# Layer 2's edge products as two float32r parts, its leaky relu as a linear sum plus one relu, and TensorE's order written out

## The chip, the cores and the metric

The kernel runs on one core of a Trainium2 chip. Its engines work side by side, each through its own queue of instructions in order: TensorE (PE, with its weight loads shown apart as PEld) writes matmul results to PSUM banks; VectorE (DVE) and ScalarE (ACT) read PSUM and SBUF; GpSimd (POOL) works on SBUF and starts some transfers; SyncE (SP) starts the others. The metric is the device time of one execution in microseconds, lower is better. Before the change it is 2248.09 us, the median of three runs (2247.92 to 2248.36).

## The reference, cut to what matters

Four graph layers run one after the other over x of 128 x 64 x 256, each followed by a residual and a layer norm. The change lies in layer 2, an attention over the 512 edges (src, dst) of a graph of 64 nodes, with 4 heads of 64 columns:

```python
Xq = (H @ W_lin.T).reshape(bt, n, h, dh)
Xv = (H @ W_val.T).reshape(bt, n, h, dh)
Qs = Xq[:, src]
Kt = Xq[:, dst]
e = jnp.einsum('behd,hd->beh', jax.nn.leaky_relu(Qs + Kt, 0.2), a)
e = e + jnp.log(A0[src, dst] + EPS)[None, :, None]
...
attn = ex / denom[src]
...
return Y @ W_out.T
```

So for every graph, edge and head a score is needed: the sum over 64 columns of a times leaky_relu(Xq[src] + Xq[dst]). The softmax over the edges of a source node and the weighted sum of Xv follow. All of it is float32.

## The kernel before, in words

The rows of x (two graphs of 64 nodes fill the 128 partitions) are held in SBUF as a tile X of NT = 64 slices. Layer 2 goes over them in K = 32 steps k of two slices i = 0, 1. The generator `scores` runs one step each time it is called on; its parts are these.

- `transposed(k)` transposes the two slices on TensorE (L2134, four 128x128 transposes into one PSUM bank of the tag "m") and DVE copies them to xT (L2136).
- `maps(k, xT)` multiplies xT by W_lin and W_val side by side (L2146, four matmuls of 128x512 into two banks "m"). ACT copies the first half of a bank to xq (L2150) and the second to xv (L2160), and SP stores xv in DRAM (L2161) for the second part of the layer.
- `edges(c)` for one half c of the 256 columns: for each slice i and each graph b of a slice, a matmul of the 64 rows of xq with the table GG (L2183), whose 512 columns hold a one at an edge's source node and a one at its target. The result is Xq[src] + Xq[dst], 128 columns on the partitions by 512 edges, in PSUM (tag "l", two tiles of two banks). ACT copies each to xs in SBUF (L2188), and DVE makes max(0.2 x, x) of it there (L2189), the leaky relu.
- `products` multiplies xs with az (L2122), the vector a spread so that each matmul adds its scores to the right rows of a bank "sc". After 16 steps a bank holds the scores of half the graphs.

The banks are shared out by pools: two for "m", four for "l", two for "sc". A bank is given to the next user in turn, who waits until the last one has been read.

The order of a step is that of the loop in `scores`. In the first steps (`apart` before, `early` after; the generator it shares the time with ends after step 14) `run(*beside)` puts pieces of layer 1's last normalization, `last_pass`, in between: ACT scales y (L2038), TensorE transposes it (L2047, into banks "m"), DVE adds it to X (L1349), takes the statistics (L1352, L1353) and, for four slices at a time, works out scale and shift (L1271 on DVE, a square root L1273 on ACT, L1274 to L1277 and L1364 on DVE), and ACT applies them (L1368, four rows). From step 15 on other work is called beside the steps: `softmax` of the first half (L2225 to L2269, which ends in scatters that POOL starts), `fetch` (L2279, M2 read back from DRAM by SP and POOL), and from step 25 on `values` (L2286 to L2329). Then layer 3 follows.

In what order an engine's instructions finally stand is decided by a scheduler, which keeps to data dependences and to the dependences added by hand: `after` makes the first product of a group wait for all of its operands, so that a wait is not met in the middle of a group, and `last` ties a group of score products behind the last edge product.

Of the kernel before, what the change touches and what calls it, by code (L numbers as in the profile page):

```python
# [7 lines left out]

F32 = mybir.dt.float32
I32 = mybir.dt.int32  # L10
# [1364 lines left out]
def tile_adj_resnorm(ctx: ExitStack, tc: tile.TileContext, I: dict, out: bass.AP, layers: int = 4):  # L1375
    nc = tc.nc
    v, s, te = nc.vector, nc.scalar, nc.tensor
# [10 lines left out]
    for b in range(2):  # L1388
        r, o = slice(b * N, (b + 1) * N), slice((1 - b) * N, (2 - b) * N)
# [9 lines left out]
    X = const.tile([P, NT, D], F32, tag="X", name="X")  # L1399
# [6 lines left out]
    ident = load("ident", [P, P], I["ident"], s)  # L1406
# [487 lines left out]
    NQ = NT // 4  # L1894
# [136 lines left out]
    def last_pass():  # L2031

        ln = Norm(nc, sy, X, 8, act=True)

        def normed(h):
            y = sy.tile([P, 2, 2 * P], F32, tag="y", name="y")
            for c in range(2):
                s.activation(y[:, c, :], Y[h // 2][:, c, h % 2 * 2 * P : (h % 2 + 1) * 2 * P], AF.Identity,  # L2038
                             bias=sh2[:, c : c + 1], scale=sc2[:, c : c + 1])
            return y  # L2040

        y = normed(0)
        for h in range(2 * NQ):
            ps = pp.tile([P, 512], F32, tag="m", name="m")
            for i in range(2):
                for c in range(2):
                    te.transpose(ps[:, i * D + c * P : i * D + (c + 1) * P], y[:, c, i * P : (i + 1) * P], ident)  # L2047
            with in_order(v, h < 3):
                ln.add(2 * h, ps, 2)
            if h == 1:  # L2050
                keep_awake(pg.tile([P, 2, 512], F32, tag="l", name="l")[:, 0, :], 2)
# [18 lines left out]
    with ExitStack() as l2:  # L2070
# [7 lines left out]
        edge_s = lt.tile([P, WE], F32, tag="edge_s", name="edge_s")  # L2078
        nc.sync.dma_start(edge_s, edge_d)
        GG, OS, lg, br, OE, ix = edge_tables(edge_s)  # L2080
        heads = lt.tile([P, 2], F32, tag="heads", name="heads")
        s.dma_start(heads, I["heads"].rearrange("p (h n) -> p h n", n=N)[:, :, 0])
        acol = lt.tile([P, 2], F32, tag="acol", name="acol")
# [9 lines left out]
        for c in range(2):  # L2093
            for h in range(2):
                o = (h + 1) * HU - 1
                v.tensor_tensor(az[:, c, o : o + 1], heads[:, h : h + 1], acol[:, c : c + 1], ALU.mult)
        bf, bb = br[:, :E], br[:, 1:]
        sc, M2 = [[None, None], [None, None]], [None, None]

        xvd = [dl.tile([P, 2, D], F32, tag=f"xv{k}", name=f"xv{k}") for k in range(NT // 2)]  # L2100

        taken, drawn, last = {}, {}, []
        beside = [iter(())]
        soft = []

        def after(ins, those, how=mybir.DependencyClass.Sync):
            for i in those:
                tc.add_manual_dep(ins.ins, i.ins.name, mybir.DependencyInfo(how, mybir.DependencyReason.DATA),
                                  reason="together")

        def products(todo, held):

            xss = [held.pop(x) for x in todo]
            mms = []
            for (k, c), (xs, _) in zip(todo, xss):
                half, u_ = divmod(k, HU)
                if u_ == 0:
                    sc[half][c] = pc.tile([P, 512], F32, tag="sc", name="sc")
                for b in range(2):
                    for i in range(2):  # L2120
                        q = 32 * (2 * b + i)
                        mms.append(te.matmul(sc[half][c][q : q + 32, :], az[:, c, HU - 1 - u_ : 3 * HU - 1 - u_],  # L2122
                                             xs[b, i], start=(u_ == 0), stop=(u_ == HU - 1)))
# [3 lines left out]
            after(mms[0], last[-1:], mybir.DependencyClass.NoSync)  # L2127

        def transposed(k):

            ps = pp.tile([P, 512], F32, tag="m", name="m")
            for i in range(2):
                for c in range(2):
                    te.transpose(ps[:, i * D + c * P : i * D + (c + 1) * P], X[:, 2 * k + i, c * P : (c + 1) * P], ident)  # L2134
            xT = sx.tile([P, 2, 2, P], F32, tag="xT", name="xT", bufs=1)
            v.tensor_copy(xT.rearrange("p i c n -> p (i c n)"), ps)  # L2136
            return xT

        def maps(k, xT, apart=False):

            xq, xv = [], sx.tile([P, 2, D], F32, tag="xv", name="xv")
            pss = [pp.tile([P, 512], F32, tag="m", name="m") for _ in range(2)]

            def product(i, cols):
                for c in range(2):
                    te.matmul(pss[i][:, cols], xT[:, i, c, :], wqv[:, c, cols], start=(c == 0), stop=(c == 1))  # L2146

            def first(i):
                xq.append(sx.tile([P, D], F32, tag="xq", name="xq", bufs=4))
                drawn[i] = s.copy(xq[i], pss[i][:, :D])  # L2150

            if apart:
                for i in range(2):
                    product(i, slice(0, D))
                    first(i)
            for i in range(2):
                product(i, slice(D, 2 * D) if apart else slice(0, 2 * D))
                if not apart:
                    first(i)
                s.copy(xv[:, i, :], pss[i][:, D:])  # L2160
            nc.sync.dma_start(xvd[k], xv)  # L2161
            return xq

        def scores():


            K = NT // 2
            xT = transposed(0)
            xq = maps(0, xT, True)
            next(beside[0])  # L2170
            next(beside[0])
            xT = transposed(1)


            held = {}

            def edges(c):
                xs, ready = {}, []
                for i in range(2):
                    pl = pg.tile([P, 2, 512], F32, tag="l", name="l")  # L2180
                    for b in range(2):
                        r = slice(b * N, (b + 1) * N)
                        mm = te.matmul(pl[:, b, :], xq[i][r, c * P : (c + 1) * P], GG[r, :], start=True, stop=True)  # L2183
                        if not b:
                            after(mm, taken.pop(i, []) + ([drawn[i]] if c == 0 else []))
                    for b in range(2):
                        x = xs[b, i] = sx.tile([P, E], F32, tag="xs", name="xs", bufs=10)
                        taken.setdefault(i, []).append(s.copy(x, pl[:, b, :]))  # L2188
                        ready.append(v.scalar_tensor_tensor(x, x, 0.2, x, ALU.mult, ALU.max))  # L2189
                held[k, c] = xs, ready  # L2190
                last.append(mm)

            for k in range(K):
                apart, xn = k < NQ, None
                edges(0)
                if apart:
                    run(*beside)
                    if k:
                        products([(k - 1, 1)], held)
                if k < K - 1:  # L2200
                    xn = maps(k + 1, xT)
                if apart:
                    run(*beside)
                elif k < K - 2:
                    xT = transposed(k + 2)
                edges(1)
# [126 lines left out]
        def run(*steps):  # L2333
            for x in steps:
                next(x, None)
# [172 lines left out]
```

## Time and profile before

| what | before |
|---|---|
| median of three runs | 2248.09 us |
| the profiled execution | 2244.9 us |
| its span, first to last instruction | 2243.1 us |
| mean granted TensorE clock | 0.995 |
| scoring of layer 2, first maps to last score products | about 1682 to 2049 us |

The profile is one execution. Its page gives busy time by engine (1), the span in 40 slices (2), the DMA queues (3), the chain of waits that ended last (4), and the costliest groups of instructions by line (5); other views cut out a stretch of time, or list instructions in order. A row "L2183 PE MATMUL l<-edge_s,xq ... x512 | 128.7, 616 | 0.4" says: line 2183, on TensorE, writing tile l from tiles edge_s and xq, 512 records, 128.7 us in which at least one of them ran, 616 ns for one, and 0.4 us of idle time of the engine in front of them. Records that overlap count once in the busy time. GG is a part of the tile edge_s and appears under that name.

### The profile page before, as it was taken

How to read it: one execution, taken by the hardware profiler on the slowest of the kernel's cores; microseconds unless marked ns; L12 is line 12 of the kernel's file. 1: busy time of each engine (PE TensorE's matmuls, PEld its weight loads, DVE VectorE, ACT ScalarE, POOL GpSimd, SP SyncE). 2: the span in 40 equal slices, each digit the busy share in tenths (PEclk: the TensorE clock that was granted, in tenths of full speed). 3: DMA queues.
4: the chain of work that ended last, by engine and by line, in shares of the span. 5: the costliest groups of instructions: out<-in, count | busy, mean ns of one | idle time of the engine just before them, and what ended most of it. 6: DMA issues, size and time to landing. Idle time of an engine off the chain costs nothing. (4 is left out here: it accounts for less than half of the span.)

```text
span 2243.1 us, 29992 instructions
## 1 busy us (share of the span) xinstructions
PE 2197.8 (98%) x8816; PEld 1211.7 (54%) x8816; DVE 1811.0 (81%) x9283; ACT 935.8 (42%) x1727; POOL 162.4 (7%) x196
## 2 busy tenths in 40 slices
PE   8999999999999999999999999999999999999997
PEld 6445665445665445665445654554434333446887
DVE  5788887888898899888899998877957777656688
ACT  1432322433322333332333322434427876567675
POOL 0111111111000000000000000000000000100631
PEclk9999999999999999999999999999999999999999
DMA  7001010111010111010111000012210100321522
GB/s 234 22 19 38 1 39 1 38 47 48 1 38 1 38 38 57 1 38 1 38 38 57 1 20 19 20 54 105 83 39 24 38 32 24 92 60 44 158 86 78
DMA packets 44667, 101.55 MB, mean 45 GB/s; under 512 B 5296, under 2 KB 23856, under 8 KB 43216
## 3 DMA queue, kind: packets, MB, share of 16 engines
q1 hardware_dynamic: 38384, 84.64, 11.0%
q0 software_dynamic: 3984, 14.40, 2.3%
q8 instruction: 70, 1.15, 0.2%
q10 hardware_dynamic: 2128, 0.54, 0.1%
q14 instruction: 101, 0.83, 0.1%
HBM read 67.97 MB, written 31.59 MB: 44 GB/s over the span
## 5 line engine op out<-in xcount | busy, mean ns | idle before, releaser
L1739 PE MATMUL pq<-H,wi 128*128 128x512 f32 (+1 forms) x1952 | 780.8, 540 | 1.5 <-ACT gate L1779 1.3
L1779 ACT ACTIVATE gate<-pq,bl 128x512 f32<-128x512 f32 (+1 forms) x504 | 315.8, 632 | 616.1 <-PE pq L1755 502.4
L1739 PEld LDWEIGHTS pq<-H,wi 128*128 128x128 f32 x1952 | 365.8, 190 | 337.5 <-issue 270.4
L1755 PE MATMUL pq<-lh,wh 128*128 128x512 f32 (+1 forms) x1152 | 462.8, 529 | 0.9 <-DVE lh L1797 0.8
L1755 PEld LDWEIGHTS pq<-lh,wh 128*128 128x128 f32 x1152 | 218.7, 190 | 203.0 <-issue 144.0
L2189 DVE SCALAR_TENSOR_TENSOR xs<-xs 128x512 f32<-128x512 f32 x256 | 165.2, 686 | 70.2 <-ACT xs L2188 69.2
L1782 ACT ACTIVATE gate<-lc 128x512 f32<-128x512 f32 (+1 forms) x144 | 83.6, 580 | 278.6 <-DVE lc L1794 103.2
L2188 ACT COPY xs<-l 128x512 f32<-128x512 f32 x256 | 134.1, 596 | 53.8 <-PE l L2183 43.8
L2183 PE MATMUL l<-edge_s,xq 64*128 64x512 f32 x512 | 128.7, 616 | 0.4 <-ACT xs L2188 0.3
L2146 PE MATMUL m<-wqv,xT 128*128 128x512 f32 (+1 forms) x264 | 121.8, 597 | 2.8 <-DVE X L1349 1.9
L2011 PE MATMUL ps<-h,w 128*128 128x512 f32 x256 | 115.9, 610 | 4.9 <-ACT h L2005 2.7
L1368 ACT ACTIVATE X<-X,ln_sh,ln_rs 128x256 f32<-128x256 f32 x187 | 97.5, 593 | 40.0 <-DVE ln_sh L1364 30.4
L1957 PE MATMUL ps<-at,w 128*128 128x512 f32 x256 | 113.2, 593 | 0.0
L802 POOL PARTITION_ALL_REDUCE qQ<-qSG x62 | 74.0, 1193 | 508.1 <-DVE pc L134 274.8
L2146 PEld LDWEIGHTS m<-wqv,xT 128*128 128x128 f32 x264 | 46.4, 189 | 76.6 <-issue 36.0
L2011 PEld LDWEIGHTS ps<-h,w 128*128 128x128 f32 x256 | 49.0, 195 | 65.7 <-issue 55.9
L1957 PEld LDWEIGHTS ps<-at,w 128*128 128x128 f32 x256 | 47.2, 190 | 52.8 <-issue 51.4
L2183 PEld LDWEIGHTS l<-edge_s,xq 64*128 64x128 f32 x512 | 44.5, 186 | 56.9 <-issue 41.7
L1352 DVE BATCH_NORM_STATS2 ln_st<-X 128x6 f32<-128x256 f32 x192 | 73.1, 416 | 1.2
L1797 DVE TENSOR_TENSOR lh<-gate 128x512 f32<-128x512 f32 (+1 forms) x72 | 43.0, 602 | 33.1 <-ACT gate L1779 33.1
L130 DVE SCALAR_TENSOR_TENSOR CS<-GA,qE 64x1 f32<-64x1 f32 x294 | 61.7, 210 | 9.5
L130 DVE SCALAR_TENSOR_TENSOR GA<-qtg,CS,GA 64x1 f32<-64x1 f32 x294 | 61.6, 210 | 8.4
(634 smaller groups left out, 3348.0 us busy)
## 6 DMA issues: line engine op xcount, KB each, us to landing
wi<-in_WihT_dram SPq DMA_DIRECT2D x16, 1024.0 KB, 4.9
wh<-in_WhhT_dram SPq DMA_DIRECT2D x12, 1024.0 KB, 6.5
xd<-X SPq DMA_DIRECT2D x16, 512.0 KB, 2.6
X<-xd SPq DMA_DIRECT2D x16, 512.0 KB, 3.4
xv<-xv SPq DMA_DIRECT2D x32, 256.0 KB, 2.0
xr<-xv POOLq DMA_DIRECT2D x32, 256.0 KB, 3.0
X<-in_x_dram SPq DMA_DIRECT2D x15, 512.0 KB, 8.8
out_dram<-X SPq DMA_DIRECT2D x15, 512.0 KB, 2.9
```

The source lines that it names most:

```text
L130: self.nc.vector.scalar_tensor_tensor(o, a, s, b, op0, op1)
L1368: nc.scalar.activation(x, x, AF.Identity, bias=sh[:, k : k + 1], scale=rs[:, k : k + 1])
L1739: te.matmul(ps, wi[:, kk, o * P : (o + 1) * P], at(kk, k), start=(kk == 0), stop=(k == 0 and kk == 1))
L1755: te.matmul(ahead[gt, c], wh[:, kk, o * P : (o + 1) * P], hst[:, kk, :M], start=False, stop=(kk == 1))
L1779: s.activation(gates[gt][:, c, :M], ps, AF.Tanh if gt == 2 else AF.Sigmoid, bias=bl[:, p - 1, o : o + 1])
L1782: s.activation(*due.pop())
L1957: te.matmul(ps, w1[:, k, c * P : (c + 1) * P], at[:, k, :], start=(k == 0), stop=(k == 1))
L2011: te.matmul(ys[c], w2[:, k, c * P : (c + 1) * P], h[:, k, :], start=(k == 2), stop=(k == 1))
L2146: te.matmul(pss[i][:, cols], xT[:, i, c, :], wqv[:, c, cols], start=(c == 0), stop=(c == 1))
L2183: mm = te.matmul(pl[:, b, :], xq[i][r, c * P : (c + 1) * P], GG[r, :], start=True, stop=True)
L2188: taken.setdefault(i, []).append(s.copy(x, pl[:, b, :]))
L2189: ready.append(v.scalar_tensor_tensor(x, x, 0.2, x, ALU.mult, ALU.max))
```

## The change

Five things are changed in layer 2.

1. The copy of the map's first half is split: ACT writes hi, the value rounded to float32r, and then the whole value; DVE subtracts and writes the rest, lo, as float32r as well. An edge product becomes two float32r matmuls that add up in one bank, lo first. GG, of zeros, ones and twos, is read as float32r.
2. leaky_relu(x) is written as 0.2 x + 0.8 relu(x). The relu is taken when a bank is read: by ACT for b = 0, by DVE for b = 1, straight from PSUM to xs, and az carries the factor 0.8. The banks "l" are now four tiles of one bank; xs has eight buffers instead of ten.
3. The linear part is a sum for each node and head: POOL multiplies the whole rows by a (spread to all partitions in arow), DVE adds up each head's 64 columns into lin. At the last step of each half `linear` scales it by 0.2 and one more matmul with GG adds it to the scores.
4. `follow` ties each of layer 2's scoring matmuls behind the TensorE instruction emitted just before it, so that they stand in the order of the program text; the tie to `last` goes.
5. In the early steps both pieces of `last_pass` that stood on either side of the maps are called after the maps.

```diff
+        GGr = GG.bitcast(F32R)
...
-                v.tensor_tensor(az[:, c, o : o + 1], heads[:, h : h + 1], acol[:, c : c + 1], ALU.mult)
+                v.scalar_tensor_tensor(az[:, c, o : o + 1], heads[:, h : h + 1], 0.8, acol[:, c : c + 1], ALU.mult, ALU.mult)
+        arow = sx.tile([P, D], F32, tag="arow", name="arow", bufs=1)
+        ps = pp.tile([P, 512], F32, tag="m", name="m")
+        for c in range(2):
+            te.matmul(ps[:, c * P : (c + 1) * P], acol[:, c : c + 1].to_broadcast([P, P]), ident, start=True, stop=True)
+        v.tensor_copy(arow, ps[:, :D])
...
+        def follow(make, *a, **k):
+            turn = next(i for i in reversed(nc.cur_bb.bb.instructions) if i.engine == te.engine)
+            ins = make(*a, **k)
+            tc.add_manual_dep(ins.ins, turn.name, mybir.DependencyInfo(
+                mybir.DependencyClass.NoSync, mybir.DependencyReason.DATA), reason="turn")
+            return ins
+
+        def linear(half, c):
+            for b in range(2):
+                r = slice(b * N, (b + 1) * N)
+                v.tensor_scalar(linb[r, c, b], lin[r, half, c], 0.2, None, ALU.mult)
+            follow(te.matmul, sc[half][c], linb[:, c].rearrange("p b i h u -> p (b i h u)"), GG, start=False, stop=False)
...
             def first(i):
-                xq.append(sx.tile([P, D], F32, tag="xq", name="xq", bufs=4))
-                drawn[i] = s.copy(xq[i], pss[i][:, :D])
+                hi = sx.tile([P, D], F32R, tag="xh", name="xh", bufs=4)
+                lo = sx.tile([P, D], F32R, tag="xl", name="xl", bufs=4)
+                drawn[i] = s.copy(hi, pss[i][:, :D])
+                whole.append(sx.tile([P, D], F32, tag="xq", name="xq"))
+                s.copy(whole[i], pss[i][:, :D])
+                v.tensor_tensor(lo, whole[i], hi.bitcast(F32), ALU.subtract)
+                xq.append((lo, hi))
...
+            weighed = sx.tile([P, 2, D], F32, tag="weighed", name="weighed", bufs=1)
+            for i in range(2):
+                nc.gpsimd.tensor_tensor(weighed[:, i, :], whole[i], arow, ALU.mult)
+            v.tensor_reduce(lin[:, k // HU, :, :, :, k % HU].rearrange("p c i h -> p i c h"),
+                            weighed.rearrange("p i (c h d) -> p i c h d", c=2, h=2), AX.X, ALU.add)
             nc.sync.dma_start(xvd[k], xv)
...
-                    pl = pg.tile([P, 2, 512], F32, tag="l", name="l")
-                    for b in range(2):
+                    pl = [pg.tile([P, 512], F32, tag="l", name="l", bufs=4) for _ in range(2)]
+                    for part, b in ((0, 0), (0, 1), (1, 0), (1, 1)):
                         r = slice(b * N, (b + 1) * N)
-                        mm = te.matmul(pl[:, b, :], xq[i][r, c * P : (c + 1) * P], GG[r, :], start=True, stop=True)
-                        if not b:
+                        mm = follow(te.matmul, pl[b], xq[i][part][r, c * P : (c + 1) * P], GGr[r, :],
+                                       start=(part == 0), stop=(part == 1))
+                        if not b and not part:
                             after(mm, taken.pop(i, []) + ([drawn[i]] if c == 0 else []))
                     for b in range(2):
-                        x = xs[b, i] = sx.tile([P, E], F32, tag="xs", name="xs", bufs=10)
-                        taken.setdefault(i, []).append(s.copy(x, pl[:, b, :]))
-                        ready.append(v.scalar_tensor_tensor(x, x, 0.2, x, ALU.mult, ALU.max))
+                        x = xs[b, i] = sx.tile([P, E], F32, tag="xs", name="xs", bufs=8)
+                        y = v.tensor_scalar(x, pl[b], 0.0, None, ALU.max) if b else s.activation(x, pl[b], AF.Relu)
+                        taken.setdefault(i, []).append(y)
+                        ready.append(y)
...
                 edges(0)
-                if apart:
-                    run(*beside)
-                    if k:
-                        products([(k - 1, 1)], held)
+                if early and k:
+                    products([(k - 1, 1)], held)
                 if k < K - 1:
                     xn = maps(k + 1, xT)
-                if apart:
-                    run(*beside)
+                if early:
+                    run(*beside * 2)
                 elif k < K - 2:
                     xT = transposed(k + 2)
                 edges(1)
                 xq = xn
-                if apart:
+                if early:
+                    products([(k, 0)], held)
                     run(*beside)
-                    products([(k, 0)], held)
                     xT = transposed(k + 2)
                     run(*beside)
```

More of the change, by code (lines that the diff above doesn't have):

```diff
@@ L9 @@
 F32 = mybir.dt.float32
+F32R = mybir.dt.float32r
 I32 = mybir.dt.int32
@@ L2050, in last_pass @@
             if h == 1:
-                keep_awake(pg.tile([P, 2, 512], F32, tag="l", name="l")[:, 0, :], 2)
+                keep_awake(pg.tile([P, 512], F32, tag="l", name="l", bufs=4), 2)
             yield
@@ L2095, in tile_adj_resnorm @@
                 o = (h + 1) * HU - 1
-                v.tensor_tensor(az[:, c, o : o + 1], heads[:, h : h + 1], acol[:, c : c + 1], ALU.mult)
+                v.scalar_tensor_tensor(az[:, c, o : o + 1], heads[:, h : h + 1], 0.8, acol[:, c : c + 1], ALU.mult, ALU.mult)
[4 more added lines that the diff above has]
+        v.tensor_copy(arow, ps[:, :D])
+        lin = sx.tile([P, 2, 2, 2, 2, HU], F32, tag="lin", name="lin", bufs=1)
+        linb = sx.tile([P, 2, 2, 2, 2, HU], F32, tag="linb", name="linb", bufs=1)
+        v.memset(linb, 0.0)
         bf, bb = br[:, :E], br[:, 1:]
@@ L2100, in tile_adj_resnorm @@
         xvd = [dl.tile([P, 2, D], F32, tag=f"xv{k}", name=f"xv{k}") for k in range(NT // 2)]
-        taken, drawn, last = {}, {}, []
+        taken, drawn = {}, {}
         beside = [iter(())]
@@ L2118, in products @@
                     sc[half][c] = pc.tile([P, 512], F32, tag="sc", name="sc")
+                if u_ == HU - 1:
+                    linear(half, c)
                 for b in range(2):
@@ L2121, in products @@
                         q = 32 * (2 * b + i)
-                        mms.append(te.matmul(sc[half][c][q : q + 32, :], az[:, c, HU - 1 - u_ : 3 * HU - 1 - u_],
+                        mms.append(follow(te.matmul, sc[half][c][q : q + 32, :], az[:, c, HU - 1 - u_ : 3 * HU - 1 - u_],
                                              xs[b, i], start=(u_ == 0), stop=(u_ == HU - 1)))
@@ L2126, in products @@
             after(mms[0], [x for _, ready in xss for x in ready])
-            after(mms[0], last[-1:], mybir.DependencyClass.NoSync)
         def transposed(k):
@@ L2133, in transposed @@
                 for c in range(2):
-                    te.transpose(ps[:, i * D + c * P : i * D + (c + 1) * P], X[:, 2 * k + i, c * P : (c + 1) * P], ident)
+                    follow(te.transpose, ps[:, i * D + c * P : i * D + (c + 1) * P], X[:, 2 * k + i, c * P : (c + 1) * P], ident)
             xT = sx.tile([P, 2, 2, P], F32, tag="xT", name="xT", bufs=1)
@@ L2139, in maps @@
         def maps(k, xT, apart=False):
-            xq, xv = [], sx.tile([P, 2, D], F32, tag="xv", name="xv")
+            xq, whole, xv = [], [], sx.tile([P, 2, D], F32, tag="xv", name="xv")
             pss = [pp.tile([P, 512], F32, tag="m", name="m") for _ in range(2)]
@@ L2145, in product @@
                 for c in range(2):
-                    te.matmul(pss[i][:, cols], xT[:, i, c, :], wqv[:, c, cols], start=(c == 0), stop=(c == 1))
+                    follow(te.matmul, pss[i][:, cols], xT[:, i, c, :], wqv[:, c, cols], start=(c == 0), stop=(c == 1))
             def first(i):
-                xq.append(sx.tile([P, D], F32, tag="xq", name="xq", bufs=4))
-                drawn[i] = s.copy(xq[i], pss[i][:, :D])
+                hi = sx.tile([P, D], F32R, tag="xh", name="xh", bufs=4)
[5 more added lines that the diff above has]
+                xq.append((lo, hi))
             if apart:
@@ L2179, in edges @@
                 for i in range(2):
-                    pl = pg.tile([P, 2, 512], F32, tag="l", name="l")
-                    for b in range(2):
+                    pl = [pg.tile([P, 512], F32, tag="l", name="l", bufs=4) for _ in range(2)]
+                    for part, b in ((0, 0), (0, 1), (1, 0), (1, 1)):
                         r = slice(b * N, (b + 1) * N)
-                        mm = te.matmul(pl[:, b, :], xq[i][r, c * P : (c + 1) * P], GG[r, :], start=True, stop=True)
-                        if not b:
+                        mm = follow(te.matmul, pl[b], xq[i][part][r, c * P : (c + 1) * P], GGr[r, :],
+                                       start=(part == 0), stop=(part == 1))
+                        if not b and not part:
                             after(mm, taken.pop(i, []) + ([drawn[i]] if c == 0 else []))
                     for b in range(2):
-                        x = xs[b, i] = sx.tile([P, E], F32, tag="xs", name="xs", bufs=10)
-                        taken.setdefault(i, []).append(s.copy(x, pl[:, b, :]))
-                        ready.append(v.scalar_tensor_tensor(x, x, 0.2, x, ALU.mult, ALU.max))
+                        x = xs[b, i] = sx.tile([P, E], F32, tag="xs", name="xs", bufs=8)
+                        y = v.tensor_scalar(x, pl[b], 0.0, None, ALU.max) if b else s.activation(x, pl[b], AF.Relu)
+                        taken.setdefault(i, []).append(y)
+                        ready.append(y)
                 held[k, c] = xs, ready
-                last.append(mm)
             for k in range(K):
-                apart, xn = k < NQ, None
+                early, xn = k < NQ, None
                 edges(0)
-                if apart:
-                    run(*beside)
-                    if k:
-                        products([(k - 1, 1)], held)
+                if early and k:
+                    products([(k - 1, 1)], held)
                 if k < K - 1:
                     xn = maps(k + 1, xT)
-                if apart:
-                    run(*beside)
+                if early:
+                    run(*beside * 2)
                 elif k < K - 2:
```

## The prediction

> **What bounds the kernel now.** I read the page first: busy time of each engine over the span, then the costliest groups.
>
> ```profile
> span 2243.1 us, 29992 instructions
> PE 2197.8 (98%) x8816; PEld 1211.7 (54%) x8816; DVE 1811.0 (81%) x9283; ACT 935.8 (42%) x1727; POOL 162.4 (7%) x196
> ...
> L2189 DVE SCALAR_TENSOR_TENSOR xs<-xs 128x512 f32<-128x512 f32 x256 | 165.2, 686 | 70.2 <-ACT xs L2188 69.2
> L2188 ACT COPY xs<-l 128x512 f32<-128x512 f32 x256 | 134.1, 596 | 53.8 <-PE l L2183 43.8
> L2183 PE MATMUL l<-edge_s,xq 64*128 64x512 f32 x512 | 128.7, 616 | 0.4 <-ACT xs L2188 0.3
> ```
>
> TensorE is busy 98% of the span, and the edge products L2183 alone take 128.7 us of it. They are 256 matmuls (32 steps, two halves c, two i, two b) and stand as 512 records: one f32 matmul is two weight loads with two streams. The pair b = 0, 1 uses 64 rows each and overlaps, so a record costs 128.7/512 = 0.25 us although it lasts 0.616.
>
> Then busy time by stage (columns: stretch, length, busy time and count of PE, PEld, DVE, ACT, POOL, clock, DMA).
>
> ```profile
> 1710.00:1750.00 40.00, 39.39 (x180) 14.61 (x177) 33.03 (x93) 31.29 (x72) 0.00 (x0) 1.00 0.05 20
> 1890.00:1920.00 30.00, 30.00 (x140) 11.92 (x136) 17.04 (x27) 17.56 (x38) 0.00 (x0) 1.00 0.07 27
> ```
>
> The change lies in layer 2's scoring (some 1680 to 2049 us), 32 steps k in two regimes. Steps k = 0 to 14 ("early") share ACT and DVE with layer 1's last normalization: both near 80%. Steps 15 to 31 ("late") leave both near 57%. PE is full in both. The timeline of an early step (start, length):
>
> ```profile
> 1735.95 3.94 PE L2146 MATMUL m<-wqv,xT 128*128 128x512 f32 x8
> 1737.19 0.66 DVE L1349 TENSOR_TENSOR X<-m,X 128x512 f32<-128x512 f32 x1
> 1737.76 0.15 DVE L1364 SCALAR_TENSOR_TENSOR ln_sh<-ln_mv,ln_rs 128x4 f32<-128x4 f32 x1
> ...
> 1737.95 2.08 ACT L1368 ACTIVATE X<-X,ln_sh,ln_rs 128x256 f32<-128x256 f32 x4 [0.42 <-DVE ln_sh L1364]
> 1739.04 0.75 DVE L1352 BATCH_NORM_STATS2 ln_st<-X 128x6 f32<-128x256 f32 x2
> 1739.70 0.30 DVE L1353 BATCH_NORM_AGGREGATE ln_mv<-ln_st 128x2 f32<-128x6 f32 x2
> 1739.82 1.99 PE L2183 MATMUL l<-edge_s,xq 64*128 64x512 f32 x8
> 1739.93 0.35 ACT L2150 COPY xq<-m 128x256 f32<-128x256 f32 x1
> 1740.18 0.37 ACT L2160 COPY xv<-m 128x256 f32<-128x256 f32 x1
> ...
> 1741.73 0.66 PE L2047 MATMUL m<-ident,y 128*128 128x128 f32 x4
> 1742.32 1.07 PE L2122 MATMUL sc<-xs,az 128*32 128x512 f32 x8
> ...
> 1747.40 3.94 PE L2146 MATMUL m<-wqv,xT 128*128 128x512 f32 x8
> ```
>
> From start to start: a step 1747.40 - 1735.95 = 11.45; maps 3.86; an edge call (8 records) 1.91; four transposes 0.59; a score product of eight records 1.00. Operations overlap their ends, so I count starts: a 512-element DVE operation 0.57 (1737.19 to 1737.76), two statistics 0.66, an ACT copy of 256 elements 0.25.
>
> **The change part by part.**
>
> *Edge products.* Each f32 matmul becomes two float32r matmuls. No float32r stands in the trace. Upper end: each costs as much as an f32 one, a call 3.83, +1.92 for each of 64 calls. In the middle: one record each, as long as an f32 record, a call 1.91, no change. Lower end: the weight loads, four in 0.30 in L2183's own row, 0.60 a call. I take 0.96: the two records say that the weights enter in two parts; the moving operand is f32 too, so I infer two parts of it within a record; a float32r product has one part on either side, a quarter of the f32 matmul and half a record. That saves 0.96 a call, 61 us in all if PE stays the bound. [...]
>
> *Drains.* Gone: 256 ACT copies (134.1 us) and 256 DVE operations (165.2). Added: 128 ACT relus (0.60 to 0.68 by L2188 and by the 0.68 of the gate rows) and 128 DVE maxima from PSUM (0.57 as the PSUM copies to xT). Net about -50 us ACT, -92 DVE, beside PE.
>
> *The split and the linear sum, for each map:* two more ACT copies of 256 (0.25 each), two DVE subtractions of 256 (0.33, from half a 512 operation plus its fixed part), two POOL products of 256 (0.70 each by L2398, seven in 4.82), one DVE reduction of 512 (0.57). At each half's end four tiny DVE scalings and, in all four times, an f32 128x512 product: 4 x 2 records x 0.43 = +3.4 us of PE. At the start two small matmuls, a copy and a memset: +1.
>
> *Order, early.* Here the sum breaks off, since the built order of the changed kernel makes a circle. On DVE the reduction waits for POOL; behind it stand, in this order, a normalization add, a drain, two statistics, a drain, an add, the xT copy, two statistics, two drains, and only then is_t, which starts the next normalization. On ACT the four X rows (L1368) stand in front of the copy that POOL's product needs. So one turn is: DVE, eight 512 operations x 0.57 + 2 x 0.66 + four aggregates x 0.08 + is_t 0.17 = 6.4; ACT's square root 0.27; five small DVE operations to ln_sh 1.0 (1678.77 to 1679.76 where they stood alone); X 1.98; copies to the second whole row 0.77 + 0.36; POOL 0.72 + 0.1; sum 11.6. PE needs only 3.86 + 2 x 0.96 + 2 x 1.0 + 3 x 0.59 = 9.6 and will wait some 2 us a step, at the layer-1 transposes that the change puts right behind the maps: their bank is free only after ACT's xv copy, behind X. So the early gain of 1.9 a step is lost whole, whatever the edge call costs up to 1.9. Ends: 11.2 (POOL without its 0.1, lighter drains) to 12.8 (drains at 0.65, POOL 1.1). [...] I take 11.8: 14 steps x 0.35 = +5.
>
> *Order, late.* No normalization is in the way. After the maps come the transposes 0.6, the edge call 0.96 and score products 2.0, so the next call's banks are asked for 3.5 us after the maps. DVE: second whole row 0.75, POOL to 1.55, reduction to 2.2, two drains to 3.4. It just fits; PE stays the bound. 17 steps x 2 calls x 0.96 = -32.6. Against it: POOL is no longer alone.
>
> ```profile
> 1936.59 1.08 POOL L2269 DMA_INDIRECT attn_d<-at,edge_s  x1 [144.87 <-DVE at L2264]
> ...
> 1949.11 2.18 POOL L2279 DMA_DIRECT2D M<-attn_d  x4 [1.80 <-DMA attn_d<-at,edge_s]
> ```
>
> The scatters keep POOL from 1936.6 to 1951.3, nothing behind it cared; now a product stands behind four of them and one behind five, the reduction waits for both, two drains behind it, then PE: +2 (0 to 5). The fetched M2 had landed by 1968 (DMA share 0.81 before, 0.04 after) for a use at 1974.8; seven shorter calls eat that slack: +1 (0 to 3). Scans and the table load of the softmax steps: +1. Late sum: -32.6 + 3.4 + 1 + 2 + 1 + 1 = -24. SP's queue has the same 32 stores of xv.
>
> *Total:* +5 - 24 = -19: 2226 against the profiled execution's 2244.9 (span 2243.1 and 1.8 around it), 2229 against the median 2248.09, which lies 3.2 above that execution.
>
> **Rivals.** *B, slower: float32r is no cheaper per record.* For it: the trace has only f32, and a float32r column is still four bytes; if the length of a stream is set by these, a record stays as it is. Against: the two-part argument. The late gain goes, the additions stay: +5 + 8.4 = +13, 2261. It decides from a call of 0.96 + 19/34 = 1.5 us; with two full records each it would be far over 2300, which I hold for unlikely (in B's chance).
> *C: the early circle does not bind.* If a turn is under PE's 9.6, another 14 x 1.9 + 5 = 32 us fall: 2198. For it, DVE would have to shed 2 us of eight rows I have; against, the order is built so. Half-way cases 2210.
> *D: the circle is wider.* Drains at 0.65 and POOL at 1.1 to 1.5 make 12.8 to 13.2: 14 x 1.4 to 1.8 = 20 to 25, total -4 to +1: 2244 to 2249, over 13.2 slower. For it: POOL's rows are of a stage with other neighbours, and the reduction's form is new. Against: L2398 was measured beside a busy DVE.
>
> **How the numbers follow.** Forecast A 0.46, B 0.17, C 0.12, D 0.25. 0.2% (4.5 us) is about what can be told from no change. A and C are faster; D splits into 0.06 faster, 0.09 the same, 0.10 slower; B is slower: 0.64, 0.09, 0.27. A's own range is 2218 to 2240. To leave out no more than 0.2 it goes down to 2208, leaving C's full gain out, and up to 2262, holding D and B without the doubled case. Time: 2229.
>
> **What would show it.** Records of float32r, one for each matmul, starts 0.12 apart (B: 0.24). An early step of 11.6 to 12 with PE idle some 2 us before the layer-1 transposes, released by ACT xv, and DVE idle in front of the subtractions and the reduction, released by ACT and POOL. A late plain step of 7.8 instead of 9.76 (maps start at 1893.06 and 1902.82). Wrong would be early steps near 9.6, or late ones that DVE or POOL end.

## The result, and the profile after

The changed kernel takes 2239.38 us, median of 6 runs (2237.52 to 2243.54), beside 2247.78 for the kernel before: a ratio of 0.9967, 95% interval 0.9954 to 0.998. That is 8 us faster, where 19 were forecast: the sign is right, the size less than half. The profiled execution of the changed kernel took 2242.81 us (span 2241.0), 3.4 above its median.

The page after (busy time, share, count; then groups: instructions, busy time, mean ns of one, idle time before them and what ended it):

```profile
PE 2161.5 (96%) x8828; PEld 1218.0 (54%) x8828; DVE 1787.6 (80%) x9261; ACT 895.2 (40%) x1663; POOL 219.3 (10%) x260
...
L2194 POOL TENSOR_TENSOR weighed<-xq,arow 128x256 f32<-128x256 f32 x64 | 57.4, 906 | 380.6 <-ACT xq L2179 380.6
L2225 ACT ACTIVATE xs<-l 128x512 f32<-128x512 f32 x128 | 71.0, 594 | 58.4 <-PE l L2124 34.5
L2225 DVE TENSOR_SCALAR xs<-l 128x512 f32<-128x512 f32 x128 | 83.7, 672 | 9.5 <-PE l L2124 5.1
...
L2180 DVE TENSOR_TENSOR xl<-xq,xh 128x256 fp32r<-128x256 f32 x64 | 31.4, 491 | 66.2 <-ACT xq L2179 66.1
...
L2124 PE MATMUL l<-edge_s,xl 64*128 64x512 f32 x256 | 60.0, 462 | 9.6 <-DVE xs L2225 7.8
```

PE sheds 36 us of busy time (2197.8 to 2161.5), yet the span falls by 2.1 in this pair: most of what PE saved became waiting. The same two windows as before (stretch, length, busy time and count of each engine, granted clock, DMA share and rate) show where:

```profile
1710.00:1750.00 40.00, 33.83 (x175) 14.63 (x175) 28.37 (x83) 26.86 (x61) 5.53 (x6) 0.96 0.05 20
1890.00:1920.00 30.00, 29.06 (x151) 13.36 (x149) 18.30 (x29) 14.81 (x37) 6.37 (x7) 1.00 0.07 27
```

In the early window PE is busy 33.8 of 40 instead of 39.4, and DVE and ACT are less busy too (28.4 and 26.9 instead of 33.0 and 31.3). No engine is full: the steps there are set by a chain of latencies. One early step of the changed kernel, from its timeline (start, length):

```profile
1737.27 3.70 PE L2124 MATMUL m<-wqv,xT 128*128 128x512 f32 x8
...
1738.72 0.16 DVE L1272 TENSOR_SCALAR is_t<-ln_mv 128x4 f32<-128x4 f32 x1
1738.91 0.20 ACT L1274 ACTIVATE is_s<-is_t 128x4 f32<-128x4 f32 x1 [1.93 <-DVE is_t L1272]
...
1740.16 2.07 ACT L1369 ACTIVATE X<-X,ln_sh,ln_rs 128x256 f32<-128x256 f32 x4 [0.49 <-DVE ln_sh L1365]
1742.14 0.35 ACT L2179 COPY xq<-m 128x256 f32<-128x256 f32 x1
...
1742.56 1.85 POOL L2194 TENSOR_TENSOR weighed<-xq,arow 128x256 f32<-128x256 f32 x2 [10.24 <-ACT xq L2179]
...
1742.81 0.66 PE L2048 MATMUL m<-ident,y 128*128 128x128 f32 x4 [1.83 <-ACT xv L2191]
1742.92 0.38 ACT L2179 COPY xq<-m 128x256 f32<-128x256 f32 x1
...
1743.39 0.50 PE L2124 MATMUL l<-edge_s,xl 64*128 64x512 f32 x2
...
1743.73 0.40 PE L2124 MATMUL l<-edge_s,xh 64*128 64x512 f32 x2
...
1743.96 0.39 PE L2124 MATMUL l<-edge_s,xl 64*128 64x512 f32 x2
...
1744.19 0.40 PE L2124 MATMUL l<-edge_s,xh 64*128 64x512 f32 x2
1744.45 0.69 DVE L2195 TENSOR_REDUCE lin<-weighed 128x8 f32<-128x512 f32 x1 [0.63 <-POOL weighed L2194]
...
1744.52 1.06 PE L2124 MATMUL sc<-xs,az 128*32 128x512 f32 x8
...
1749.36 1.13 PE L2124 MATMUL m<-wqv,xT 128*128 128x512 f32 x2
```

Read it as one turn: square root, X rows on ACT, the copy to xq behind them, POOL's products, DVE's reduction, and from there through DVE to the next is_t. From maps to maps it is 12.09 (before: 11.45), and PE waits 1.83 in front of the layer-1 transposes. The edge call is in there as well: pairs of row halves start at 1743.39, .73, .96, 1744.19, and the next operation at 1744.52: 1.13 in all.

By stages, from starts of the same operations in both traces; the forecast's terms are put to the stage in which they fall (of the 34 late calls one stands in the second, 20 in the third, 13 in the fourth):

| stage | before | after | change | forecast |
|---|---|---|---|---|
| start of the span to the second 512-column maps | 1701.07 | 1700.80 | -0.3 | +1 |
| 14 early steps | 161.10 | 170.38 | +9.3 | +4 |
| 10 late steps, to the maps before the values | 104.63 | 95.03 | -9.6 | -14.5 |
| to the second softmax's transposes | 90.68 | 83.97 | -6.7 | -9.8 |
| from there to the end | 185.6 | 190.8 | +5.2 | 0 |

The last row was in no sum. A late wait, and then the place of the last row, in the timeline of PE:

```profile
1945.93 0.51 PE L2124 MATMUL l<-edge_s,xl 64*128 64x512 f32 x2 [2.66 <-DVE xs L2225]
...
2104.82 1.61 PE L2341 MATMUL m<-mc,xr 64*64 64x64 f32 x32 [3.47 <-DMA xr<-xv]
2106.36 6.27 PE L2364 MATMUL ps<-wo,yT 128*128 128x256 f32 x16
```

At 2104.82 PE has waited 3.47 for a load of xr, and what follows is slow, at a granted clock of 0.50 to 2109.76 and 0.67 to 2112.47: 16 products in 6.27, which take 3.72 in e4 (below).

### The profile page after: what moved, and what is told of

It reads as the page before. It is cut to its first block, busy times and chain, and to the rows that moved or that the text cites. A ratio compares the mean times of both kernels' runs of the same rounds, so it can differ in the third digit from the quotient of the medians.

```text
span 2241.0 us, 30079 instructions
## 1 busy us (share of the span) xinstructions
PE 2161.5 (96%) x8828; PEld 1218.0 (54%) x8828; DVE 1787.6 (80%) x9261; ACT 895.2 (40%) x1663; POOL 219.3 (10%) x260
## 3 DMA queue, kind: packets, MB, share of 16 engines
q8 instruction: 70, 1.15, 0.2%
## 5 line engine op out<-in xcount | busy, mean ns | idle before, releaser
L1369 ACT ACTIVATE X<-X,ln_sh,ln_rs 128x256 f32<-128x256 f32 x187 | 97.4, 592 | 42.3 <-DVE ln_sh L1365 28.4
L2194 POOL TENSOR_TENSOR weighed<-xq,arow 128x256 f32<-128x256 f32 x64 | 57.4, 906 | 380.6 <-ACT xq L2179 380.6
L2225 ACT ACTIVATE xs<-l 128x512 f32<-128x512 f32 x128 | 71.0, 594 | 58.4 <-PE l L2124 34.5
L2225 DVE TENSOR_SCALAR xs<-l 128x512 f32<-128x512 f32 x128 | 83.7, 672 | 9.5 <-PE l L2124 5.1
L2180 DVE TENSOR_TENSOR xl<-xq,xh 128x256 fp32r<-128x256 f32 x64 | 31.4, 491 | 66.2 <-ACT xq L2179 66.1
L2124 PE MATMUL l<-edge_s,xl 64*128 64x512 f32 x256 | 60.0, 462 | 9.6 <-DVE xs L2225 7.8
```

The costliest lines, as they stand in the source:

```text
L1369: nc.scalar.activation(x, x, AF.Identity, bias=sh[:, k : k + 1], scale=rs[:, k : k + 1])
L2124: ins = make(*a, **k)
L2194: nc.gpsimd.tensor_tensor(weighed[:, i, :], whole[i], arow, ALU.mult)
L2225: y = v.tensor_scalar(x, pl[b], 0.0, None, ALU.max) if b else s.activation(x, pl[b], AF.Relu)
```

## The experiments

All ratios are against the kernel before, with 95% intervals.

**e1: the X rows behind the copies.** Only the order on ACT changes.

```
-                xn = maps(k + 1, xT)
+                xn = maps(k + 1, xT); [after(r(), [s_last[0]], NoSync) for r in held_rows]; held_rows.clear()
...
-                    ln.flush()
+                    ln.flush(held=held_rows if 4 <= h < 2 * NQ - 1 else None)
```

> The changed kernel with one change of order: in the early steps the four X rows of layer 1's normalization stand behind the copies of the maps on ACT instead of in front of the second one. Theory (the circle DVE, square root, X rows, copies, POOL product, reduction sets the early step): the copies no longer wait for the normalization, the circle is open, and the step falls from 12.09 to PE's own 10.0 to 10.4: 14 x 1.7 to 2.1 = 24 to 29 us, 2210 to 2216 against 2239, with PE's 1.84 us wait in front of the layer-1 transposes gone. Rival (DVE's or POOL's own work, or the xv copy's place, sets the step): it stays at 11.5 or more, 2231 to 2240.

2209.42 us, 0.9823 (0.981 to 0.9837), 30 below the changed kernel. Timeline of an early step:

```profile
1750.01 3.70 PE L2124 MATMUL m<-wqv,xT 128*128 128x512 f32 x8
...
1753.55 0.60 PE L2048 MATMUL m<-ident,y 128*128 128x128 f32 x4
...
1754.28 0.39 ACT L2191 COPY xv<-m 128x256 f32<-128x256 f32 x1
...
1754.55 2.08 ACT L1369 ACTIVATE X<-X,ln_sh,ln_rs 128x256 f32<-128x256 f32 x4
...
1757.56 0.50 PE L2124 MATMUL l<-edge_s,xl 64*128 64x512 f32 x2 [0.26 <-DVE ln_mv L1354]
...
1759.88 0.70 PE L2124 MATMUL m<-wqv,xT 128*128 128x512 f32 x1
```

The transposes follow the maps without a wait, the step is 9.87, and PE's longest wait in it is 0.26. Nothing but the order was changed, so the circle through the X rows is shown.

**e2: without the linear sum.**

```
-                nc.gpsimd.tensor_tensor(weighed[:, i, :], whole[i], arow, ALU.mult)
-            v.tensor_reduce(lin[...], weighed.rearrange(...), AX.X, ALU.add)
...
-                    linear(half, c)
```

> The changed kernel without the linear sum: no POOL products, no reductions, no scalings and none of the four f32 linear products, so the scores lack their linear part; the split and its order stay. Theory (circle): the way back to DVE is by the subtraction of the second half, and POOL's 0.9 + 0.1 and the reduction's 0.57 leave the circle while 0.4 of the subtraction comes in: early step 12.09 to about 11.0, 14 x 1.1 = 15 us; the four products 3.4; the wait of 2.66 behind the scatters and some of 0.9 a late step: together -20 to -24, 2215 to 2219. Rival (PE's wait comes from the X rows on ACT alone, POOL's sum is hidden beside it): early step 11.9 to 12.1, -5 to -8, 2231 to 2234.

2216.39 us, 0.9861 (0.9845 to 0.9876). Early steps are 11.09 to 11.13, with a wait of 1.55 still in front of the transposes, behind ACT's xv: the circle goes back by the subtraction, as the theory has it (from the second one at 1749.38, released by ACT, DVE runs without a gap to is_t at 1755.60), and without POOL's products and the reduction it is 1.0 shorter. The wait of 2.66 behind the scatters is gone.

**e3: edge products in f32.**

```
-                v.tensor_tensor(lo, whole[i], hi.bitcast(F32), ALU.subtract)
-                xq.append((lo, hi))
+                xq.append((whole[i],))
...
-                for part, b in ((0, 0), (0, 1), (1, 0), (1, 1)):
+                for part, b in ((0, 0), (0, 1)):
-                    mm = follow(te.matmul, pl[b], xq[i][part][r, c * P : (c + 1) * P], GGr[r, :], ...)
+                    mm = follow(te.matmul, pl[b], xq[i][part][r, c * P : (c + 1) * P], GG[r, :], ...)
```

> The changed kernel with the edge products in f32 on one whole row, as before: no split, no subtraction, one copy for each map row; the linear sum, the single drains and the order stay. Theory (a float32r call saves 0.72 against 1.91, and only where PE is the bound): late steps longer by 2 x 0.72, 34 x 0.72 = +24 us less some 3 to 5 of waits that DVE's lost subtractions end; the early circle, shorter by a copy and a subtraction, falls under PE's own 11.5, so early steps 11.5 to 11.7 instead of 12.17: -7 to -9; together +10 to +16, 2249 to 2255. Rival (the products gain nothing by float32r once their ends are counted): late steps as they are, 2228 to 2236.

2250.33 us, 1.0012 (1.0003 to 1.0021). A late plain step is 9.94 instead of 8.41, and the first, which holds a linear product, 10.1 instead of 8.60: float32r pays there. Early steps are 10.96, PE full, against 12.09 of the changed kernel: its faster products stand in a slower step. The total lies in the forecast by luck: the 14 early steps are 16.8 shorter, where 7 to 9 were expected, and what comes behind them is longer than expected. Its page gives POOL's product with no subtraction beside it:

```profile
L2194 POOL TENSOR_TENSOR weighed<-xq,arow 128x256 f32<-128x256 f32 x64 | 46.5, 729 | 392.8 <-ACT xq L2176 392.8
```

**e4: the second fetch of M2 on one queue.**

```
-                    (nc.sync, nc.gpsimd)[b].dma_start(
+                    (nc.sync, nc.sync if half else nc.gpsimd)[b].dma_start(
```

> The changed kernel with the second fetch of M2 wholly on SP's queue, so that the loads of xr on POOL's queue are not behind half of it. Theory (PE's 3.47 us at 2101, released by the xr load, comes from that load standing behind 2 MB of M2 in the same queue, and the lower clock after it): the wait goes, -3 to -6 us, 2233 to 2236. Rival (the transfer engines are full with M2 whatever the queue): the wait stays or moves to the first use of M2's second half, 2237 to 2243.

2238.06 us, 0.9958 (0.9944 to 0.9972): the intervals overlap, so the time is not told from the changed kernel's. In its trace the wait is no longer for the load:

```profile
2100.04 3.72 PE L2364 MATMUL ps<-wo,yT 128*128 128x256 f32 x16
...
2107.20 0.98 PE L2341 MATMUL m<-mc,xr 64*64 64x64 f32 x32 [0.76 <-ACT mc L2321]
```

The xr wait of 3.47 is 0.76, for ACT. In e1 and e3, with the fetch on two queues, PE waits 2.46 and 3.52 in this place.

**e5: e1, with the late reduction behind the drains and e4's fetch.**

```
-            v.tensor_reduce(lin[...], ...)
+            summed[:] = [lambda: v.tensor_reduce(lin[...], ...)]; k > NQ or summed.pop()()
...
-                xq = xn
+                xq = xn; [after(r(), held[k, 1][1][-1:], NoSync) for r in summed]; summed.clear()
```

> e1 with two more changes: from step 16 on the reduction of the linear sum stands behind the two drains of the edge call instead of in front of them, and the second fetch of M2 is wholly on SP's queue as in e4. Theory (DVE waits for POOL in front of drains that PE needs: 2.65 us behind the scatters, 0.9 at 1864.9 of e1's trace and smaller ones; and 2.46 at the xr load): these waits go and with them lower clock after them, -5 to -8 against e1's 2209.4, 2201 to 2204. Rival (POOL's scatters are not what ends that wait, the drains are late through the softmax scans): the wait of 2.65 stays, 2206 to 2209.

2204.77 us, 0.9813 (0.98 to 0.9826). The step behind the scatters is 8.42 instead of e1's 11.78, so that wait was DVE standing behind POOL. The forecast is missed by a little; another wait stands in the trace, which e1's does not have:

```profile
1934.45 0.37 ACT L2191 COPY xv<-m 128x256 f32<-128x256 f32 x1 [4.77 <-DMA xv<-xv]
...
1934.87 0.93 PE L2124 MATMUL m<-ident,X 128*128 128x128 f32 x4 [4.16 <-ACT xv L2191]
```

ACT may not overwrite xv until its store has landed, and the store stands behind the first fetch of M2.

**e6: one part only, on e1.**

```
-                for part, b in ((0, 0), (0, 1), (1, 0), (1, 1)):
+                for part, b in ((1, 0), (1, 1)):
```

> e1 with one part only: the products with the low part are left out (the scores lose precision; the split and its subtraction are still made, the low part is unused), so an edge call is four float32r products instead of eight. What an edge call costs. Theory (ends: a pair of row halves costs 0.235, and beginning and ending a call 0.1 each, whatever the type): call 0.2 + 2 x 0.235 = 0.67 against 1.12. Rival (all of the call is by the product, 0.14 each): 0.56. The step falls by 2 x 0.45 where PE stays the bound: 64 x 0.45 = -29, 2181, or 2190 where DVE (some 8.9 busy in a step of 9.87) takes over in the early steps.

PE's timeline at a late step:

```profile
1862.98 0.60 PE L2124 MATMUL m<-ident,X 128*128 128x128 f32 x4
1863.51 0.73 PE L2124 MATMUL l<-edge_s,xh 64*128 64x512 f32 x4
1864.17 1.93 PE L2124 MATMUL sc<-xs,az 128*32 128x512 f32 x16
```

The call takes 1864.17 - 1863.51 = 0.66, as the theory of the ends has it (0.67), not 0.56. The time is 2200.33 us, 0.9796 (0.9781 to 0.9811): 9 less than e1's, where 19 to 28 less were expected. Early steps are 9.63, with a wait of 0.72 for DVE in front of an edge call in each: DVE's order becomes the bound 0.24 under e1's step. The expectation had DVE as the next bound, but at 8.9.

**e7: the split alone, in the kernel before.**

```
-                        mm = te.matmul(pl[:, b, :], xq[i][r, c * P : (c + 1) * P], GG[r, :], start=True, stop=True)
+                        mm = te.matmul(pl[:, b, :], xq[i][part][r, ...], GG.bitcast(F32R)[r, :], start=(part == 0), stop=(part == 1))
```

> The kernel before with the split alone: edge products in two float32r parts, a second copy and a subtraction for each map row; the ACT copy and the DVE operation for each product, no linear sum and no given order stay. Theory (float32r saves PE 0.72 to 0.79 a call; late steps have room on ACT and DVE): late -1.45 x 17 = -24; early ACT and DVE, near 80% of 11.45, get 0.6 and 0.9 more and stay under it, PE's own step falls to 9.9, and the circle through the copies keeps most of it: 11.0 to 11.5, 0 to -6; together 2217 to 2224, better than the whole change. Rival (without the single drains DVE takes over, or the products stand between the maps' and each call begins and ends more often): early 11.5 to 12.5, late -0.8 a step: 2235 to 2250.

2221.57 us, 0.9889 (0.9874 to 0.9904): one part of the change earns 25 us, the whole of it 8. Busy time in 100 us of early steps, first the changed kernel:

```profile
1720.00:1820.00 100.00, 85.00 (x442) 37.36 (x438) 68.82 (x198) 67.71 (x157) 14.78 (x16) 0.95 0.06 24
```

and the split alone:

```profile
1720.00:1820.00 100.00, 98.95 (x494) 41.09 (x494) 91.28 (x266) 93.21 (x222) 1.82 (x3) 1.00 0.09 32
```

The split alone keeps three engines over 90% and makes steps of 10.3 (two in 20.7); the changed kernel has far less to do on DVE and ACT, fills none, and takes 12.1.

**e8: the pieces as before, one in front of the maps.**

```
-                edges(0)
+                edges(0); run(*beside * early)
...
-                    run(*beside * 2)
+                    run(*beside)
```

> The changed kernel with the layer-1 pieces placed as before, one in front of the score products and the maps and one behind the maps, instead of both behind; all else stays. Theory (the early step is set by the circle through ACT's X rows and POOL's sum, not by where PE's transposes stand): early step 12.0 to 12.2, 2236 to 2242. Rival (the wait in front of the transposes is made by putting them right behind the maps): it goes, early step 11.0 to 11.5, 2226 to 2231.

2243.8 us, 0.9986 (0.9977 to 0.9995). Neither: where the granted clock is 0.99 (1780 to 1820) the step is 11.62, so the place of the transposes is worth 0.47 of a step, but the wait only moves, to an edge call, and the circle stays. In about half of the early steps the clock falls (a mean of 0.93 over 1720 to 1820), and these are 13.0 to 13.2 long. A window with two falls in it, and a wait in the timeline of PE:

```profile
1720.00:1760.00 40.00, 34.59 (x165) 15.22 (x166) 27.05 (x77) 24.74 (x58) 5.78 (x6) 0.89 0.05 20
```

```profile
1795.83 0.50 PE L2124 MATMUL l<-edge_s,xl 64*128 64x512 f32 x2 [1.53 <-DVE xs L2225]
```

**e9: e5, with the late stores of xv on ACT's queue.**

```
-            nc.sync.dma_start(xvd[k], xv)
+            (s if k > NQ else nc.sync).dma_start(xvd[k], xv)
```

> e5 with the late stores of xv (steps over 16) issued on ACT's queue instead of SP's. In e5's trace PE waits 4.16 us at 1934.87 for ACT's copy to xv, and ACT waits 4.77 for an earlier store of xv, which stands on SP's queue behind the first fetch of M2. Theory (the queue): on a queue of its own the store lands within some 3 us, PE's wait of 4.16 and the lower clock behind it (0.75 in 1936 to 1941) go: -4 to -6 against e5's 2204.8, 2199 to 2201. Rival (all transfer engines are full with M2 until 1934, the store lands late on any queue): the wait stays at 3 to 4, 2203 to 2206.

2200.8 us, 0.9801 (0.9788 to 0.9814), the fastest of those that leave nothing out, 46 us under the kernel before. (The interval overlaps e5's, though each of its runs is under e5's fastest, 2203.64.) In the stretch around the fetch the stores land after 10.2 us at most, where e5 has up to 18.1. The wait of 4.16 is gone and the transposes follow the maps:

```profile
1931.92 0.60 PE L2124 MATMUL m<-ident,X 128*128 128x128 f32 x4
...
1933.07 0.33 ACTq L2197 DMA_DIRECT2D xv<-xv  x1
```

**e10: the split alone, with the X rows behind the copies.** The edits of e1 and e7 together.

> e7 (the kernel before with the split alone) with the X rows behind the copies, as in e1. What the linear sum with its single drains and the given order earn once the circle is open: e1 has 2209.4. Theory (with the copies first, e7's early steps fall from 10.35 to DVE's or PE's 9.9 to 10.2, the late steps stay; what is left of the linear sum is its shorter drains against POOL's sum, the reduction and four products, which about balance): 2213 to 2219, so the linear sum earns 4 to 10. Rival (the single drains are what makes early steps of 9.87 possible): early step stays 10.3 or more, 2219 to 2224, and the linear sum earns 10 to 15.

2221.81 us, 0.9892 (0.9877 to 0.9907), as e7. Two early steps take 21.5 here and 19.7 in e1. Busy time in 100 us of early steps, e10 and then e1:

```profile
1720.00:1820.00 100.00, 96.79 (x482) 39.67 (x482) 90.69 (x255) 89.74 (x215) 1.81 (x3) 1.00 0.09 32
```

```profile
1720.00:1820.00 100.00, 97.41 (x530) 44.84 (x523) 85.39 (x246) 80.12 (x193) 18.81 (x23) 1.00 0.11 40
```

PE is nearly full in both, so what differs is its own time: 10.4 busy us a step in e10, 9.6 in e1, for the same products. e10 and e7 lack the given order (points 4 and 5 of the change), and in their timelines edge products stand between parts of the maps, so that more groups begin and end. By the time, the rival holds: e1 is 12 us ahead, once the circle is open. But this is the linear sum with its single drains and the given order together, and the trace points to the order: PE's own work makes 0.8 of the 0.9 by which the step is longer. The same is seen without float32r: over the 14 early steps PE is busy 159.1 us in the kernel before and 153.3 in e3, which has the given order. No run has the split with the given order alone, so what the linear sum earns by itself is not shown.

## Why the prediction was right in sign and wrong in size

*Edge products, "I take 0.96".* This is the step that failed: the term of the sum that was mis-sized most. The argument (a float32r product is a quarter of an f32 one) holds: a pair of row halves starts every 0.235 (1743.73 to .96 to 1744.19), where f32 needs two streams of 0.43. But I halved the whole call, and a call has two ends that were not shortened with the type. They stood in the trace before:

```profile
1739.81 0.30 PEld L2183 LDWEIGHTS l<-edge_s,xq 64*128 64x128 f32 x4 [0.76 <-issue]
...
1740.35 0.19 PEld L2183 LDWEIGHTS l<-edge_s,xq 64*128 64x128 f32 x2 [0.24 <-ACT xq L2150]
...
1740.78 0.19 PEld L2183 LDWEIGHTS l<-edge_s,xq 64*128 64x128 f32 x2 [0.23 <-issue]
```

Its streams, which start at 1739.82 and then with these weight loads, are 0.53, 0.43 and 0.43 apart, and the next operation starts 0.52 later: 4 x 0.43 + 0.2 = 1.92. By that the float32r call is 0.2 + 4 x 0.235 = 1.14; measured 1.13. e6 shows the ends: half the products take 0.66, not half of 1.13. For the 33 calls of the two late rows that is 33 x 0.17 = 5.6 us of missing gain. A late plain step took 8.41, where 7.8 was forecast; in five such steps the second call takes 1.26 instead of 1.13, but there its weight loads wait for ACT's relus:

```profile
1905.65 0.21 PEld L2124 LDWEIGHTS l<-edge_s,xl 64*128 64x128 f32 x2 [0.92 <-ACT xs L2225]
...
1906.24 0.21 PEld L2124 LDWEIGHTS l<-edge_s,xl 64*128 64x128 f32 x2 [0.27 <-ACT xs L2225]
```

In e7 and e10 the call takes 1.13 in this place and the step 8.18, so these waits cost 0.23 a step, another 1.2 us. The two late rows lack 4.9 and 3.1; that the sum of 6.8 comes near this is partly luck, for other misses cancel: the wait of 2.66 and the maps behind it at a clock of 0.67 cost 4.3 (forecast +2), a linear product takes 1.06 instead of 0.86, and a wait of 1.98 that the kernel before has at 1886.78 is gone, which no term counted. That a float32r product has one part on either side was my inference from the two records of an f32 matmul. Each float32r matmul has one record (256 from xl); the streams agree with a quarter (0.235 against 0.86, a ratio of 0.27), the call does not agree with the half that was taken (1.13 against 1.91, a ratio of 0.59).

*Order, early, "taken 11.8".* The circle was there, with the parts and the wait that were named: e1 opens it and the step is PE's own but for 0.26, e2 takes POOL out of it and it shrinks by 1.0. Measured 12.09, 0.29 over the value taken and inside its ends. The part that was too small is mainly POOL: from the end of ACT's copy at 1743.30 to the reduction at 1744.45 is 1.15, and 0.72 + 0.1 was set; the rest of the turn is 10.94, where 10.8 was summed. I priced a product at 0.70 by L2398, which runs with no subtraction beside it; e3 has 0.73 in this very place without one, the changed kernel 0.94 (median of its early steps). The 14 steps cost +9.3 and not +4: half of that miss lies in the first 13 steps, half in the last, which took 12.47 (a wait of 1.84, then a clock of 0.72 over 1865.0 to 1871.2) where the kernel before has 10.37. The 0.2 by which 11.8 lies over the sum of 11.6 was an estimate that no run shows as a term of its own; in its place the turn is 0.33 longer at POOL and 0.14 in the rest: the row should have been taken with its neighbours.

*Order, late.* The wait behind the scatters was there, 2.66 (forecast +2; e5 shows the cause). The other, 1.30 before the first use of M2 (forecast +1), has the size but not the cause that was named: the transfer engines, full until 1969 (DMA share 0.94 from 1966), are idle from 1969.5 to 1970.5 (0.00), so the fetch had landed, and PE waits at 1974.63 for ACT's copy of it, which starts at 1973.52 behind two relus. In e3, with its slow calls, the same wait is 1.30 too. "It just fits; PE stays the bound" held for steps of 8.41 but for 0.23 and failed for others by up to 0.90, before an edge call, released by DVE.

*Outside the sum.* The xr load that stood behind the fetch: 3.47, and a lower clock after it (0.50 in the next 3.4 us). On POOL's queue the kernel before issued loads of xr at 2083.83 and 2092.48, in front of its part of the fetch at 2094.05; in the changed kernel that part stands at 2089.17, and the next loads follow at 2094.03 and 2097.40. e4 removes the wait from the trace; its worth in the median stays open.

*Rivals.* B (no cheaper per record) falls by the starts of 0.235. C (the circle does not bind) falls by PE's waits and by e1. D (12.8 to 13.2) is not reached at a clock of 1.00, where the step is 12.09. The drains came out near their forecast (63 us less on ACT, 82 less on DVE, for 50 and 92). That they earn nothing in the changed kernel is argued, not shown: what they free on DVE and ACT is not what the early step waits for, but four of DVE's stand in the circle, and no run of the changed kernel has the old ones.

## What to carry to other kernels

Before pricing a cheaper product, split its call into streams and ends by the starts of its records; here only the streams scaled (0.86 to 0.235 for a pair of row halves; the ends of a call stayed 0.2). When a change adds a side path that comes back to an engine's queue, follow the order of the queues around once: if it closes a circle, less work on TensorE, DVE and ACT need not shorten a step (here 12.09 after 11.45), and moving one group in one queue can be worth more than the change (here 30 us against 8). When a stage gets faster, look at the order in which small transfers stand to large ones on each queue: the load of xr here (a wait of 3.47), and the store of xv in e5 (4.77), became waits behind a fetch of M2.

## What the runs showed of the hardware

- *POOL and DVE.* POOL's 256-element product takes 0.73 without the subtraction beside it (e3) and 0.91 on average in the changed kernel; the subtraction takes 0.42 without POOL (e2) and 0.49 there.
- *The clock.* In the changed kernel's trace a stretch of 3.4 us with PE busy for 1.56 is followed by one at a granted clock of 0.54, then by one at 1.00:

```profile
1715.90:1719.30 3.40, 1.56 (x8) 0.77 (x8) 0.84 (x2) 3.40 (x10) 1.18 (x2) 0.96 0.00 0
1719.30:1722.70 3.40, 3.40 (x17) 1.04 (x15) 2.77 (x8) 2.05 (x4) 0.66 (x1) 0.54 0.21 80
1722.70:1726.10 3.40, 3.40 (x29) 1.93 (x26) 3.35 (x10) 2.18 (x4) 0.00 (x0) 1.00 0.00 0
```

  Only some steps with the same wait lose clock: after the wait of 1.84 that ends at 1718.37 the clock falls to 0.54, after the one of 1.84 that ends at 1803.79 it is 1.00 (1803.8 to 1807.2). In the changed kernel a step that loses it (12.98) is nearly made up by the next (11.48); in e8 it is not. e2, with waits of 1.55 in each step, keeps 1.00 over 100 us. What decides which steps are hit no run shows, and what a filled gap would change was not tried.
